# A two-layer graph network kernel: U1 and U2 loaded by SyncE, the activation table loaded ahead, attention sums in groups of two tiles, accumulators taken one by one

## The chip, the cores and the metric

The kernel runs on one core of one Trainium2 chip. The metric is the device time of one execution in microseconds (us), the median of several runs. A profiled execution gives the trace from which single durations are read.

The engines are named as in the profile: PE is TensorE (PEld its weight loads), DVE is VectorE, ACT is ScalarE, POOL is GpSimd, SP is SyncE, which here does nothing but issue DMA transfers. ACT can issue DMAs too (ACTq in the timelines).

## The reference

There are N = 3327 nodes with D = 256 features, an adjacency matrix `adj` (about 0.5% filled, with a full diagonal), and two layers. Each starts with a layer norm and a relu and adds its output to x.

```python
# layer 0, on h = relu(layernorm(x)); Xf = Xa = h, Z = 0
R = adj + I;  R = R / R.sum(-1)
for n in range(2):
    q = Xa @ W1.T @ W2.T;  k = Xa @ W3.T          # 64 wide
    A = softmax(q @ k.T), cut to the largest entries that hold 0.9 of the row, renormalised
    Xf = R @ Xf;  Xa = A @ Xa
    Z += Xf @ U1[n].T + Xa @ U2[n].T
x += layernorm(h + Z) * ln_g + ln_b
# layer 1, on h = relu(layernorm(x)): graph attention, 4 heads of 64 features
hp = h @ W;  s, d = hp @ a_src, hp @ a_dst         # one of each per node and head
e = leaky_relu(s[i] + d[j], 0.2), only where adj[i, j] > 0
x += elu(softmax(e) @ hp)
```

## The kernel before

The rows are padded to 3328 and cut into NT = 26 tiles of 128. The function `fast` does the work; a second path, `general`, is entered only when a check at the end asks for it, which it doesn't for these inputs.

**The order of the work.** Nearly everything goes through a `Plan` (L470 to L567). A step is put into it with `put(engine, length, rank, function, needs, take, give, lag)`: the engine that runs it, an assumed length, a rank (the lowest goes first among the steps that are ready), the steps that it needs, and the buffers that it takes and gives back by name. `order()` plays these steps through as a list schedule on the assumed lengths, and `issue()` then emits the instructions in that order. What comes out is a fixed order for every engine. On the chip each engine runs its list in order, and a wait at the head of the list holds all that stands behind it. A changed rank, length or buffer thus may shift the order anywhere after it.

**The start.** `weights()` (L689 to L726) is called ahead of the plan, and issues on ACT's queue the DMAs of W1 (L696), W2 (L697), W3 twice (L699) and, in a loop over the two steps, the halves of U1 (L702) and U2 (L703), 256 KB each. The tiles of x (128 KB each, L1818) are issued by SP. `deviations` then takes the mean and the variance of each tile on DVE (L1134, L1135) and turns them into scale and offset on POOL (L1139 to L1142). `prepare` follows tile by tile: ACT's relu (L1160, with scale and offset), PE's transposes (L1165), a copy by DVE (L1168), PE's projection on queries and keys (L1173), and ACT's copy of it into a `kq` buffer (L1179; there are three). Out of `kq` POOL copies keys and queries (L1182, L1183) and SP starts a DMA (L1186) that doubles the queries onto other partitions. `keys_summed` (L762 to L783) sums statistics of the keys on PE, DVE and ACT. `project_u` (L1203 to L1215) multiplies every tile by U1 (PE at L1209, four records for a tile), and its two results are copied by ACT (L1212) and DVE (L1213).

**Layer 0.** For each row tile of each step, PE makes logits (L873), ACT their exponents (L887) and a first guess of the threshold (L907 to L910), then `density` (four activations on one column, L914 to L917) and `count` (passes of 3.07 us over 3327 columns, L924). POOL refines the threshold from the counts (`step`, L941 to L970), DVE sorts a window around it and drops what lies below (L979 to L1034), and PE transposes (L1047) and multiplies (L1059) what is left; ACT copies the transposes (L1052). The products with R are made by PE in between (`Full`, L1091), with one PSUM accumulator `accf`, and copied by ACT (L1098). The steps of a row are put into the plan by `search` (L1410 on), where density has the row's rank − 2.05, and the first counts − 2.1.

**Layer 1.** `attend_neighbours` (L1500 to L1811) goes through four blocks of W = 832 target columns. In each block it loops over the 26 source tiles j. ACT makes a 0/1 mask from the adjacency (L1623, L1624), DVE makes the masked exponents of the four heads (L1635, four instructions per tile) into one of seven `e` buffers (four named e, three called e2 in the plan), and PE uses them twice: for the products with the features (L1651, an array tiling of 128×64) into two accumulators of two PSUM banks each (`pl`, all of that pool), and for the sums (L1665, tiling 128×32) into `acca` and `accf`. Sums of JG = 3 tiles are run together after the products of the third. An e buffer is given back by the sums.

At the end of a block, `leave` has ACT copy both accumulators (L1711) and the sums (L1714) into an e buffer. Then seven times PE transposes a piece (L1732), DVE takes the reciprocals (L1736), ACT makes the elu's parts (L1744), and DVE adds (L1748, L1749). Those steps run beside the next block. The next block's first product takes both accumulators and needs `evacuated`, the second of the two copies. The last block ends in a variant of its own.

```python
x_ = plan.put("PE", 1.42, rank, product, 0, needs=[x_, last_acc, evacuated], take=["pl", "pl"] * (j == 0))
last_acc = plan.put("PE", 1.42, rank, product, 1, needs=[x_, y_])
group.append((sums, mine))
if len(group) == JG or j == NT - 1:
    for n_, (fn, name) in enumerate(group):
        last_den = plan.put("PE", 1.42 + 0.2 * (n_ == 0), rank, fn, needs=[last_acc, last_den], ...
```

Of the kernel before, what the change touches and what calls it, by code (L numbers as in the profile page):

```python
# [10 lines left out]
F32 = mybir.dt.float32  # L11
# [3 lines left out]
AF = mybir.ActivationFunctionType  # L15
# [4 lines left out]
P = 128  # L20
# [550 lines left out]
def fast(  # L571
# [17 lines left out]
    nc = tc.nc  # L589
    V, S, T, GP = nc.vector, nc.scalar, nc.tensor, nc.gpsimd  # L590
# [21 lines left out]


    powers = const.tile([P, 4], F32, name="powers")
    adds = const.tile([P, 2], F32, name="adds")
    for k, v in enumerate((-0.5, 0.5, -1.0, 0.25)):
        GP.memset(powers[:, k : k + 1], v)
    for k, v in enumerate(QUANTILE[1:3]):
# [12 lines left out]
    with ExitStack() as l0:  # L631
# [57 lines left out]
        def weights():  # L689
            held = {}  # L690
            w1 = etpool.tile([P, 4, P], F32, name="et")
            w1 = w1[:, 0, :].rearrange("p (c o) -> p c o", c=2)
            w2 = small.tile([P, PIECES, 8], F32, name="cands").rearrange("p c r -> p (c r)")[:DA, :DA]
            w1r = small.tile([P, PIECES * 8], F32, name="rest", bufs=1)[:DA].rearrange("p (k o) -> p k o", k=1)
            w1r = [w1r[:, 0, :], small.tile([P, P], F32, name="kq", bufs=BUFS["kq"])[:DA]]
            nc.scalar.dma_start(w1, w1t.rearrange("(c p) o -> p c o", p=P))  # L696
            nc.scalar.dma_start(w2, w2t)  # L697
            for r in range(2):
                nc.scalar.dma_start(wqk[:, :, r, r * DA : r * DA + DA], w3t.rearrange("(c p) o -> p c o", p=P))  # L699
            for n in range(STEPS):  # L700
                cols = slice((1 - n) * D, (2 - n) * D)
                nc.scalar.dma_start(u1[:, :, cols], u1t[n].rearrange("(c p) o -> p c o", p=P))  # L702
                nc.scalar.dma_start(u2[:, :, cols], u2t[n].rearrange("(c p) o -> p c o", p=P))  # L703

            def turn():
                held["ps"] = ps_x.tile([DA, 2, P], F32, name="px")
                for k in range(2):
                    T.transpose(held["ps"][:, k, :], w1[:, k, :], ident)

            def copy():  # L710
                for k in range(2):
                    S.copy(w1r[k], held["ps"][:, k, :])

            def product():
                held["ps"] = ps_x.tile([P, 2, DA], F32, name="px")
                for k in range(2):
                    T.matmul(held["ps"][:, k, :], w1r[k], w2, start=True, stop=True)

            def place():
                for r in range(2):  # L720
                    S.copy(wqk[:, :, r, (1 - r) * DA : (2 - r) * DA], held["ps"])

            a = plan.put("PE", 0.25, -200.0, turn, take=["px"], needs=[plan.put("SP", 0.02, -201.0, lambda: None, lag=8.0)])
            a = plan.put("ACT", 0.5, -200.0, copy, needs=[a], take=["kq"], give=["px"])
            a = plan.put("PE", 0.25, -200.0, product, needs=[a], take=["px"], give=["kq"])
            return plan.put("ACT", 0.5, -200.0, place, needs=[a], give=["px"])  # L726
# [476 lines left out]
        def project_u(t, rank):  # L1203
            held = {}

            def product():
                ps = held["ps"] = ps_x.tile([P, 2 * D], F32, name="px")
                for k in range(2):
                    T.matmul(ps, c[:, t, k * P : (k + 1) * P], u1[:, k, :], start=(k == 0), stop=(k == 1))  # L1209

            a = plan.put("PE", 1.75, rank, product, needs=[turned_h[t], weighed], take=["px"])
            b = plan.put("ACT", 0.37, -2.6, lambda: S.copy(main[:, t, :D], held["ps"][:, :D]), needs=[a])  # L1212
            e = plan.put("DVE", 0.43, -2.6, lambda: V.tensor_copy(c[:, t, :], held["ps"][:, D:]), needs=[a])  # L1213
            plan.put("SP", 0.0, -2.6, lambda: None, needs=[b, e], give=["px"], lag=0.0)
            return b, e  # L1215
# [194 lines left out]
        def search(row, rank, keys, stats_of, fresh):  # L1410


            n, i = row.n, row.i
            got, a = [], None
            for g in range(2):

                def logits(g=g):
                    row.logits(2 * g)
                    row.logits(2 * g + 1)

                a = plan.put(
                    "PE", 2.1 - 0.7 * g, rank - 2.5, logits, needs=[keys, fresh, a], take=["pl", "pl"] + ["e", "sc"] * (1 - g)
                )
                for k in (2 * g, 2 * g + 1):
                    got.append(
                        plan.put("ACT", 1.15 if k < 3 else 0.5, rank - 2.5, row.exps, k, needs=[a], give=["pl"])
                    )
            row.pieces = dict(logits=a)
            a = plan.put("ACT", 0.35, rank - 2.4, row.row_sum, needs=[got])
            a = plan.put("POOL", 1.3, rank - 2.4, row.root, needs=[a, stats_of])  # L1430
            a = row.pieces["guess"] = plan.put("ACT", 1.0, rank - 2.4, row.guess, needs=[a])
            more = plan.put("ACT", 0.85, rank - 2.05, row.density, needs=[a])
            for j in range(2):
                got = [
                    plan.put("ACT", 3.05, rank - (2.1, 1.7)[j], row.count, j, fn, needs=[a])
                    for fn in (AF.Relu, AF.Sign)[j:]
                ]
                a = plan.put("POOL", (3.8, 4.7)[j], rank - (2.0, 1.6)[j], row.step, j, GP, needs=[got, more])
            if EVALS[n] == 3:
                a = row.pieces["counted"] = plan.put("ACT", 3.05, rank - 1.4, row.count, 2, AF.Sign, needs=[a])  # L1440
                a = plan.put("DVE", 2.7, rank - 1.3, row.step, 2, V, needs=[a])
            halves = []
            for h in range(2):
                for part in range(2):
                    a = plan.put(
                        "DVE", 3.2 - 2.0 * part, rank - 1.0, row.window, h, part, needs=[a], take=["y"] * (1 - part),
                        give=["y"] * part, lag=0.02, hold=1.95 * (1 - part),
                    )
                    halves.append(a)
            may = plan.put("POOL", 0.8, rank - 1.5, row.free, needs=[halves[2]])  # L1450
            a = plan.put("DVE", (1.8, 2.5)[n], rank - 1.0, row.sort, needs=[a])
            a = plan.put("DVE", 3.1, rank - 1.0, row.choose, needs=[a, may], take=["cum"])
            total = plan.put("POOL", 1.2, rank - 1.0, row.total, needs=[a], give=["cum"])
            drops = []
            for o in range(4):
                a = plan.put("DVE", 1.03, rank - 1.0, row.drop, o, needs=[a], hold=1.0)
                drops.append(a)
            return total, drops
# [41 lines left out]
        def attend_neighbours(rows, ends, done, fulls):  # L1500
# [1 line left out]

            W = NP // 4
            C = W // 2
            JG = 3
            logits_done = [r.pieces["logits"] for r in rows]
            freed = [p for p in done]
            extra = {}
# [65 lines left out]

            last, f_ = {}, None
            used_heads = [None, None]
            evacuated = None
            both = broadcast(0, 59.5)
            for b in range(4):
                lo = b * W  # L1580
                r0 = 60.0 + 10.0 * b
                q = {}
                tiles = range(lo // P, lo // P + 7)
                off = lo - tiles[0] * P

                def open_acc(q=q):
                    q["acc"] = [ps_l.tile([P, 2, 512], F32, name="pl") for _ in range(2)]

                def open_den(q=q):
                    q["den"] = [ps_a.tile([P, 512], F32, name=n) for n in ("acca", "accf")]  # L1590
# [3 lines left out]
                for j in range(NT):  # L1594
# [48 lines left out]

                    def product(a, j=j, held=held, q=q, open_acc=open_acc):

                        if j == 0 and a == 0:
                            open_acc()
                        for c in range(2):
                            for k in range(2):
                                h = 2 * a + k  # L1650
# [27 lines left out]
                    else:  # L1678
# [10 lines left out]
                    y_ = plan.put("DVE", 2.1, rank, exponents, 1, needs=[x_, both[1]], give=own, hold=2.0)  # L1689
                    last_e = y_  # L1690
                    x_ = plan.put(
                        "PE", 1.42, rank, product, 0, needs=[x_, last_acc, evacuated], take=["pl", "pl"] * (j == 0)
                    )
                    last_acc = plan.put("PE", 1.42, rank, product, 1, needs=[x_, y_])
                    group.append((sums, mine))
                    if len(group) == JG or j == NT - 1:
                        for n_, (fn, name) in enumerate(group):
# [16 lines left out]
                            S.copy(q["ot"][:, 2, c], q["den"][c][:, :C])  # L1714

                r1 = r0 + 9.0
                evacuated = a = plan.put("ACT", 0.9, r1, leave, 0, needs=[last_acc], take=["e"], give=["pl"])
                evacuated = a = plan.put("ACT", 0.9, r1, leave, 1, needs=[a], give=["pl"])
                out_of = plan.put("ACT", 1.1, r1, leave, 2, needs=[a, last_den], give=["acca", "accf"])
                for x0 in range(0, W, P):  # L1720
                    m = min(P, W - x0, N - lo - x0)
# [95 lines left out]
        def load_x(t):  # L1817
            nc.sync.dma_start(rhs[0][:, t, :], x[t * P : (t + 1) * P, :])  # L1818

        weighed = weights()  # L1820
        loads = [plan.put("SP", 0.58, -200.0 + t, load_x, t) for t in range(NT)]
        measured = {}
# [136 lines left out]
```

## Time and profile before

| | |
|---|---|
| median of 3 runs | 2219.33 us |
| lowest and highest | 2218.48, 2220.72 us |
| profiled execution, its own time | 2222.8 us |
| its span in the trace | 2221.0 us |
| PE busy | 2171.0 us, 98% of the span |
| DVE busy | 1613.7 us, 73% |
| ACT busy | 1442.5 us, 65% |
| POOL busy | 931.3 us, 42% |
| mean granted TensorE clock | 0.998 |

The times in the timelines count from the start of the span. A group's duration is the time from its first start to its last end, so it can hold gaps between its instructions; the ends of matmuls are modelled. The bracket behind an instruction names the idle time of its engine just before, and what ended it. Layer 1's four blocks open on PE at 1720, 1847.90, 1967.31 and 2086.16 us, and the last sums end at 2205.02.

### The profile page before, as it was taken

To read this page: it belongs to the slowest core of one execution; us is meant where nothing else is said; L and a number is where in the kernel's file an instruction comes from. 1 tells how busy PE (TensorE), PEld (TensorE's weight loads), DVE (VectorE), ACT (ScalarE), POOL (GpSimd) and SP (SyncE) were. 2 spreads that over 40 slices of the span, in tenths; PEclk is the share of its full clock that TensorE was granted. 3 is DMA by queue.
4 is the path that set the end of the run, shared out by engine and by line. 5 is a ranking of instruction groups with operands and counts; after the bars stand their busy time and mean duration, and the time that the engine had idled before them with its cause. 6 is when DMAs were issued, how large, how long until landed. Compare 5 with 4: busy or idle time off the path is not lost.

```text
span 2221.0 us, 35941 instructions
## 1 busy us (share of the span) xinstructions
PE 2171.0 (98%) x11978; PEld 1535.2 (69%) x11978; DVE 1613.7 (73%) x4229; ACT 1442.5 (65%) x2725; POOL 931.3 (42%) x2210
## 2 busy tenths in 40 slices
PE   7999999999999999999999999999999999999997
PEld 5388778777887788877878788887887433333333
DVE  5576656546655744277879877888777997989896
ACT  5766676567566661478888777878774455465553
POOL 5564455535544541256656666566653200000001
PEclk9999999999999999999999999999999999999999
DMA  4012121212212232622222222222225344444341
GB/s 120 1 45 80 52 71 54 71 52 62 71 54 71 71 91 67 189 82 60 63 58 63 62 72 74 80 62 64 67 77 152 117 130 143 116 137 126 107 127 50
DMA packets 192323, 183.75 MB, mean 83 GB/s; under 512 B 15386, under 2 KB 146176, under 8 KB 192128
## 3 DMA queue, kind: packets, MB, share of 16 engines
q1 hardware_dynamic: 190144, 180.10, 28.1%
q8 instruction: 96, 1.57, 0.3%
q10 hardware_dynamic: 1984, 1.26, 0.2%
q14 instruction: 99, 0.81, 0.1%
HBM read 164.41 MB, written 15.94 MB: 81 GB/s over the span
## 4 chain that ended last, share of the span: by engine, by line
PE 71%; issue 9%; ACT 8%; POOL 5%; DVE 5%; DMA 2%; SPq 0%; ACTq 0%; DVEq 0%; POOLq 0%
PE acca L1059 20%; PE accf L1091 20%; PE pl L1651 9%; PE pl L873 6%; ACT junk L924 6%; PE px L1047 6%; PE acca L1665 2%; PE accf L1665 2%; PE px L1258 2%; PE px L1209 1%; PE px L1354 1%; POOL sc L937 1%; ACT et L1052 1%; DVE e L1635 1%; PE px L1236 1%
## 5 line engine op out<-in xcount | busy, mean ns | idle before, releaser
L1059 PE MATMUL acca<-rhs,et 128*128 128x256 f32 x2704 | 620.7, 380 | 1.7 <-ACT et L1052 1.6
L924 ACT ACTIVATE junk<-e,sc 128x3327 fp8e5<-128x3327 f32 x182 | 559.1, 3072 | 48.0 <-POOL sc L969 46.6
L1059 PEld LDWEIGHTS acca<-rhs,et 128*128 128x128 f32 x2704 | 499.4, 191 | 66.0 <-ACT et L1052 4.8
L1091 PE MATMUL accf<-c,at 128*128 128x256 f32 x1352 | 313.5, 382 | 6.1 <-ACT f L1098 6.1
L1091 PE MATMUL accf<-main,at 128*128 128x257 f32 x1352 | 310.3, 381 | 3.0 <-DMA at<-in_adjt_dram 2.8
L979 DVE SCALAR_TENSOR_TENSOR y<-e,sc 128x1664 f32<-128x1664 f32 x104 | 208.1, 2001 | 127.1 <-POOL sc L966 125.1
L1052 ACT COPY et<-px 128x512 f32<-128x512 f32 (+1 forms) x364 | 192.6, 553 | 142.0 <-PE acca L1059 83.4
L1091 PEld LDWEIGHTS accf<-c,at 128*128 128x128 f32 x1352 | 250.0, 190 | 48.3 <-ACT f L1098 10.9
L1091 PEld LDWEIGHTS accf<-main,at 128*128 128x128 f32 x1352 | 251.0, 190 | 44.9 <-issue 6.5
L984 DVE MAX8 cands<-y 128x8 f32<-128x208 f32 x832 | 242.4, 361 | 3.6
L1034 DVE SCALAR_TENSOR_TENSOR e<-e,thr 128x832 f32<-128x832 f32 x208 | 212.9, 1079 | 2.0
L887 ACT ACTIVATE e<-pl 128x1024 f32<-128x1024 f32 x208 | 179.0, 863 | 37.6 <-PE pl L873 36.9
L1624 ACT ACTIVATE et<-at 128x448 bf16<-128x448 f32 (+1 forms) x204 | 112.3, 550 | 137.4 <-DVE e L1635 81.6
L1047 PE MATMUL px<-ident,e 128*128 128x128 f32 x1352 | 191.4, 274 | 7.1 <-ACT et L1052 2.3
L1784 POOL TENSOR_TENSOR qq<-qq 128x256 f32<-128x256 f32 x4 | 3.0, 755 | 453.7 <-ACT qq L1780 453.7
L1047 PEld LDWEIGHTS px<-ident,e 128*128 128x128 f32 x1352 | 160.1, 141 | 47.0 <-issue 11.8
L1651 PE MATMUL pl<-e,main 128*64 128x416 f32 x1024 | 187.2, 515 | 0.0
L873 PE MATMUL pl<-kt,qq 64*128 64x512 f32 (+1 forms) x832 | 173.5, 535 | 0.0
L1651 PEld LDWEIGHTS pl<-e,main 128*64 128x64 f32 x1024 | 71.1, 137 | 107.3 <-issue 91.9
L1635 DVE SCALAR_TENSOR_TENSOR e<-c,low,et 128x832 f32<-128x832 f32 x128 | 128.6, 1073 | 7.9 <-PE accf L1665 3.6
L873 PEld LDWEIGHTS pl<-kt,qq 64*128 64x128 f32 x832 | 71.6, 186 | 83.9 <-issue 77.9
L1635 DVE SCALAR_TENSOR_TENSOR e<-qq,low,et 128x832 f32<-128x832 f32 x120 | 120.4, 1076 | 2.6 <-ACT e L1711 2.0
(527 smaller groups left out, 3083.9 us busy)
## 6 DMA issues: line engine op xcount, KB each, us to landing
at<-in_adjt_dram SPq DMA_DIRECT2D x414, 256.0 KB
at<-in_adjt_dram SPq DMA_DIRECT2D x102, 192.0 KB
at<-in_adjt_dram SPq DMA_DIRECT2D x52, 128.0 KB
ys<-ystage SPq DMA_DIRECT2D x26, 256.0 KB
rhs<-in_x_dram SPq DMA_DIRECT2D x26, 128.0 KB
ystage<-in_x_dram SPq DMA_DIRECT2D x26, 128.0 KB
base<-ys SPq DMA_DIRECT2D x26, 128.0 KB
x1s<-ystage SPq DMA_DIRECT2D x26, 128.0 KB
```

The lines of the kernel that those rows point to most:

```text
L873: T.matmul(pl[:, r, :m], qq[half, self.i, :], kt[half, 512 * k : 512 * k + m], start=True, stop=True,)
L887: S.activation(self.e[:, 1024 * k : 1024 * k + 2 * w].rearrange("p (r w) -> p r w", r=2), pl, AF.Exp, accum_out=(self.p0, self.p1, self.p2 ...
L924: S.activation(junk[:, :N], self.e[:, :N], fn, bias=t, scale=-1.0, accum_out=dst, saturate=False)
L979: V.scalar_tensor_tensor(self.y[:, : hi - lo], self.e[:, lo:hi], self.up, self.e[:, lo:hi], ALU.is_lt, ALU.mult, accum_out=(self.h0, self. ...
L984: V.max(self.cands[:, o // PIECE, :], self.y[:, o - lo : min(o + PIECE, hi) - lo])
L1034: V.scalar_tensor_tensor(piece, piece, self.thr[:, o : o + 1], piece, ALU.is_gt, ALU.mult)
L1047: T.transpose(pt[:, k, :], self.e[:, j * P : (j + 1) * P], ident)
L1052: S.copy(self.et[g][:, :m, :], self.pt.pop(g)[:, :m, :])
L1059: T.matmul(self.acc, et[:, j - 4 * g, :], rhs[self.n][:, j, :], start=(j == 0), stop=(j == NT - 1))
L1091: T.matmul(self.acc[:, : self.w], self.at[j // JC][:, j % JC, :], self.src[:, j, : self.w], start=(j == 0), stop=(j == NT - 1),)
L1635: V.scalar_tensor_tensor(held["e"][:, k, :], extra["both"][b % 2][:, k, :], low[:, j, k : k + 1], held["mask"], ALU.max, ALU.mult,)
L1651: T.matmul(q["acc"][a][k * FH : (k + 1) * FH, c, :C], main[:, j, h * FH : (h + 1) * FH], held["e"][:, h, c * C : (c + 1) * C], start=(j == 0),
```

## The change

There are six edits. The loads of U1 and U2 become steps of the plan on SP: U1's two halves with ranks −196.5 and −195.5 among the loads of x (−200 to −175), U2's with rank −150 behind them; `project_u` needs these loads of U1 now and no longer `weighed`, the placing of the projection's weights. ACT gets one activation with Exp on one column straight after its four remaining DMAs, ahead of the plan's steps. Density's rank goes from −2.05 to −2.2. JG goes from 3 to 2. The accumulators are opened, taken and waited for one by one: product 0 of a block's first tile needs the first copy, product 1 the second.

In the order that the plan puts out, SP has four loads of x, U1, one of x, U1, 21 of x, and then U2 twice, ahead of the first doubling DMA. ACT has the four DMAs, the table load, the Exp and then the first relu. In layer 1, blocks 1 to 3 begin with two tiles of products ahead of the first sums, and go on in groups of two.

```diff
-    adds = const.tile([P, 2], F32, name="adds")
+    adds = const.tile([P, 3], F32, name="adds")
@@ weights()
             for n in range(STEPS):
                 cols = slice((1 - n) * D, (2 - n) * D)
-                nc.scalar.dma_start(u1[:, :, cols], u1t[n].rearrange("(c p) o -> p c o", p=P))
-                nc.scalar.dma_start(u2[:, :, cols], u2t[n].rearrange("(c p) o -> p c o", p=P))
+                uloads.append(
+                    plan.put(
+                        "SP", 0.4, -196.5 + n, nc.sync.dma_start, u1[:, :, cols],
+                        u1t[n].rearrange("(c p) o -> p c o", p=P), lag=8.0,
+                    )
+                )
+                plan.put(
+                    "SP", 0.4, -150.0, nc.sync.dma_start, u2[:, :, cols], u2t[n].rearrange("(c p) o -> p c o", p=P)
+                )
+
+            S.activation(adds[:, 2:], powers[:, :1], AF.Exp)
@@ project_u()
-            a = plan.put("PE", 1.75, rank, product, needs=[turned_h[t], weighed], take=["px"])
+            a = plan.put("PE", 1.75, rank, product, needs=[turned_h[t], uloads], take=["px"])
@@ search()
-            more = plan.put("ACT", 0.85, rank - 2.05, row.density, needs=[a])
+            more = plan.put("ACT", 0.85, rank - 2.2, row.density, needs=[a])
@@ attend_neighbours()
-            JG = 3
+            JG = 2
-            evacuated = None
+            evacuated = [None, None]
-                q = {}
+                q = {"acc": {}}
-                def open_acc(q=q):
-                    q["acc"] = [ps_l.tile([P, 2, 512], F32, name="pl") for _ in range(2)]
+                def open_acc(a, q=q):
+                    q["acc"][a] = ps_l.tile([P, 2, 512], F32, name="pl")
-                        if j == 0 and a == 0:
-                            open_acc()
+                        if j == 0:
+                            open_acc(a)
-                        "PE", 1.42, rank, product, 0, needs=[x_, last_acc, evacuated], take=["pl", "pl"] * (j == 0)
+                        "PE", 1.42, rank, product, 0, needs=[x_, last_acc, evacuated[0]], take=["pl"] * (j == 0)
                     )
-                    last_acc = plan.put("PE", 1.42, rank, product, 1, needs=[x_, y_])
+                    last_acc = plan.put(
+                        "PE", 1.42, rank, product, 1, needs=[x_, y_, evacuated[1]], take=["pl"] * (j == 0)
+                    )
-                evacuated = a = plan.put("ACT", 0.9, r1, leave, 0, needs=[last_acc], take=["e"], give=["pl"])
-                evacuated = a = plan.put("ACT", 0.9, r1, leave, 1, needs=[a], give=["pl"])
+                first = plan.put("ACT", 0.9, r1, leave, 0, needs=[last_acc], take=["e"], give=["pl"])
+                a = plan.put("ACT", 0.9, r1, leave, 1, needs=[first], give=["pl"])
+                evacuated = [first, a]
@@ fast()
+        uloads = []
         weighed = weights()
```

## The prediction, made before the result was known

> **What bounds the kernel now.** I read the split of busy time over stretches of the span first. Its columns are the stretch in us, its length, then busy time and instruction count of PE, PEld, DVE, ACT and POOL, then granted clock, DMA share and GB/s. The cuts are the first relu's end on PE (10.76), the first attention (110), layer 1 (1720) and its blocks.
>
> ```profile
> 0.00:10.76 10.76, 0.00 (x0) 0.00 (x0) 2.70 (x10) 1.94 (x3) 5.79 (x33) 1.00 0.77 227
> 10.76:110.00 99.24, 91.68 (x400) 53.38 (x401) 57.46 (x216) 71.41 (x167) 55.12 (x152) 1.00 0.15 43
> 110.00:1720.00 1610.00, 1593.42 (x8089) 1293.03 (x8087) 1103.02 (x3462) 1109.01 (x1938) 852.38 (x2008) 1.00 0.26 73
> 1720.00:1847.90 127.90, 127.28 (x910) 54.44 (x910) 122.49 (x155) 62.84 (x130) 11.88 (x10) 1.00 0.44 130
> 1847.90:1967.31 119.41, 118.05 (x857) 43.84 (x853) 110.18 (x126) 64.88 (x162) 0.00 (x0) 1.00 0.44 130
> ```
>
> TensorE is the bound nearly everywhere: 1593.42 of 1610 us in layer 0's body, 118.05 of 119.41 in block 1. Free time is there in two places: the first 10.76 us, where PE does nothing, and the busy but stretched starts of blocks 1 to 3. So I next read ACT's, POOL's and SP's timelines of the start (start, duration, engine, line; a bracket is idle time and its releaser).
>
> ```profile
> 6.03 0.38 ACTq L702 DMA_DIRECT2D late<-in_u1t_dram  x1
> 8.30 0.40 ACTq L703 DMA_DIRECT2D u<-in_u2t_dram  x1
> 8.81 1.28 ACT L1160 ACT_TABLE_LOAD   x1 [8.81 <-DMA u<-in_u2t_dram]
> 10.11 2.08 ACT L1160 ACTIVATE rhs<-rhs,mvs 128x256 f32<-128x256 f32 x4
> ```
>
> ```profile
> 5.11 0.24 POOL L1142 TENSOR_SCALAR mvs<-mvs 128x1 f32<-128x1 f32 x1
> ```
>
> ```profile
> 0.72 16.47 SPq L1818 DMA_DIRECT2D rhs<-in_x_dram  x26
> 17.44 28.72 SPq L1186 DMA_DIRECT2D qq<-kq  x26
> ```
>
> POOL has tile 0's deviation at 5.35, but ACT's first relu starts at 10.11: it stands behind eight DMAs, of which the last two wait in the queue (6.03, 8.30), and a table load. The third thing to read is PE's and DVE's timeline in layer 1.
>
> ```profile
> 1847.90 2.32 PE L1651 MATMUL pl<-e,main 128*64 128x416 f32 x12
> ...
> 1907.21 5.81 PE L1651 MATMUL pl<-rhs,main 128*64 128x416 f32 x32
> ...
> 1920.07 8.60 PE L1651 MATMUL pl<-e,main 128*64 128x416 f32 x48
> ...
> 1932.93 1.27 PE L1651 MATMUL pl<-c,main 128*64 128x416 f32 x6
> ```
>
> ```profile
> 1860.16 2.08 DVE L1635 SCALAR_TENSOR_TENSOR e<-c,low,et 128x832 f32<-128x832 f32 x2 [1.31 <-PE accf L1665]
> ```
>
> ```profile
> 1978.95 2.08 DVE L1635 SCALAR_TENSOR_TENSOR e<-qq,low,et 128x832 f32<-128x832 f32 x2 [0.59 <-PE accf L1665]
> ```
>
> A cycle of three tiles lasts 1920.07 − 1907.21 = 12.86 us. At a block's start DVE stops for want of an e buffer until the first sums have run.
>
> **What the Trainium skill says.** "ScalarE: Activation LUTs", What ACT_TABLE_LOAD costs: about 1283 ns, and 1380 ns of drain. The trace agrees on the load (1.28 us); it shows no drain behind it, the relu follows in 0.02 us. "DMA: Bandwidth & Descriptors", Issuing engines are not separate DMA queues: transfers from any engine end on the same 16 DMA engines, and moving the issue saves only sequencer time. Here an issue is 0.38 to 0.48 us, but the gaps 6.03 to 8.30 show that ACT stood far longer, so I count the gaps too. "TensorEngine Tiling (Array Packing)", Key Properties: a change of tiling mode drains TensorE. The trace lets me price that below: products are 128×64, sums 128×32.
>
> **The change, part by part.** The profiled execution took 2222.8 us (span 2221.0, 1.8 outside it), 3.5 above the median of 2219.33; I carry differences over unchanged.
>
> *U off ACT, table first.* ACT's queue keeps four weight loads (0.47 + 0.53 + 1.11 us, over by 2.91), the 1.28 load and a [128×1] Exp, about 0.2 (the [128×1] activations L914 to L917 take 0.19 to 0.21). All that ends near 4.5, before POOL's 5.35, so relu 0 goes from 10.11 to about 5.4. Each later step gains less, because each has its own feeder: relus 2 and 3 wait for POOL's 8.63; POOL's next round (12.62, it waited 4.00 for DVE) moves up 4.0. PE could start 4.7 us earlier; that is the upper end. On SP, two U1 DMAs now stand among the x loads, and two U2 DMAs behind them: before the first doubling of the keys (L1186) there are 30 issues in place of 26. The 26 issues of x fill 16.47 us with gaps, as x tiles are awaited too; at the closer spacing of 0.475 us (0.72, 1.18, 1.64, 2.12) the four would cost 1.9 us alone. These doublings hold the three kq buffers for about 2 us each (the first x took from 0.72 to statistics at 3.14, 2.42 us). By hand: U2 issued by 15.8, first doubling about 16.0 and landed at 18.0, in place of 17.44 and the fourth key share (L1179) at 21.29. That gives 3.3 us, which I take: **−3.3**. Lower end: 0, if SP's issues with the U's in them run no faster than now. U1 is first used at 26.33 (L1209) and lands long before.
>
> *Density ahead of the counts.* The diff also moves the rank of density (L914 to L917) below that of the count passes. On ACT four short activations, 67.03 to 67.66, go ahead of a 3.07 us pass. The first row's count then ends 0.6 later, but POOL's step, which waited 1.04 for density at 67.73, need not. So −0.5 to +0.6; taken 0.
>
> *Sums by two tiles.* A tile's products are 16 records, about 2.8 us, its sums 16, about 1.4. A group of three is 12.86, 4.287 a tile. The last group of a block before holds two (26 = 8×3 + 2): 1839.23 to 1847.90 is 8.67, 4.335 a tile. Solving 3t + s = 12.86 and 2t + s = 8.67 gives t = 4.19 and s = 0.29 for one round trip between tilings. Groups per block go from 9 to 13, so 4 × 4 × 0.29 = **+4.6**; counting runs in the emitted order instead, 30 more at 0.147 each, +4.4. I take +4.5. PE is the bound here, nothing hides it: DVE needs 4 × 0.996 = 3.98 us a tile, less than 4.34.
>
> *The block's start.* Of block 1's 119.41 us, products and sums are 26 × 4.19 = 108.9, the 21 transposes 2.3 (six take 0.81 from start to start at 1968.86, with one change of tiling in it), and 28 runs at 0.147 are 4.1: 115.3 in all. The remaining 4.1 is stretch (3.6 in blocks 2 and 3, 118.85 and 118.86 long). Its cause is in the two DVE lines: the fifth exponents start at 1978.95, 11.6 us after the block opened at 1967.31, because the sums which give the first e buffer back were at 1977.28. With groups of two the emitted order has the first sums behind two tiles' products in place of three, by hand 6.7 to 7.2 us after the opening, 3.3 earlier. What comes late next is DVE itself: it has 110.8 us of work per block, against 116 to 117. I leave 1.3 of stall in each: 2.8 + 2.3 + 2.3 = **−7.4**. Bounds: −11.3 (all of it) and 0.
>
> *Accumulators one by one.* The two copies of the accumulators (L1711) run 1843.69 to 1844.54 and 1845.09 to 1845.94, and the sums after the last product hold PE until 1847.90; the next block's first product finds both banks free. With two tiles still 2 × 1.39 = 2.8 us of sums cover them. **0**; if the cover were gone, a copy of 0.85 saved at each of three boundaries, −2.6. Block 0 starts without a stall and stays so, as does the 16 us tail after 2205.02.
>
> *The body.* The planner orders all engines anew, so waits will move. PE idles 16.6 us of 1610 there, most where a copy on ACT is late (6.4 us over 9 waits on L1098). Taken 0, bounds −5 and, below, +11.
>
> Sum: −3.3 + 0 + 4.5 − 7.4 + 0 = −6.2, so 2219.33 − 6.2 = 2213.1 (profiled: 2222.8 to about 2216.6).
>
> **The rivals.** (A) *More of the same*: the stall goes whole (−11.3 + 4.5 = −6.8), and the body's waits may shrink too: 2219.33 − 3.3 − 6.8 = 2209.2, to 2206 with 3 from the body. For it: the body has 16.6 us to give. Against: PE's waits there have several releasers. (B) *Groups of two cost and give nothing*: at the block's start DVE waits next for ACT's elu (a 3.38 us wait on L1744 at 1973.72 is in the trace), the 4.5 us stay: 2219.33 − 3.3 + 4.5 = 2220.5. Against: the e buffer is what was awaited last. (C) *The early start is hidden*: the doublings on SP are no earlier, PE waits for keys: 2219.33 − 2.9 = 2216.4. (D) *Slower*: ACT in the body. A copy (L1098, L1052) that is ordered behind a 3.07 us count pass, because density's new rank shifted the order, holds PE's only accumulator accf. Fourteen more such waits at today's mean of 6.4/9 = 0.7 are +10 and outweigh the 6.2 from the ninth on; with +11 the time is 2224.1. For it: ACT is 69% busy in the body and each of 52 rows is moved. Against: density is a fifth of a pass, and the row's order stays the same.
>
> **How the numbers follow.** About 0.2%, 4.4 us, is what a measurement of this kernel can tell from no change: faster is below 2214.9, slower above 2223.8. Forecast 0.48 (own range 2209 to 2217: 0.34 faster, 0.14 same); A 0.12, all faster; B 0.15 (0.02, 0.11, 0.02 by what the start gives); C 0.12 (0.04, 0.08, 0); D 0.13 (0, 0.01, 0.12). Sums: 0.52, 0.34, 0.14. The range of 2206 to 2222 leaves out D's most and little of A.
>
> **What would show it.** First relu at 5.4 and PE's first matmul near 6; first doubling near 16. In layer 1 a cycle of 8.67 us for two tiles; blocks 1 to 3 near 117.8, 117.7 and 117.7 long; the wait of DVE on accf at a block's start below 1.5 us. I am wrong if blocks exceed 119.4 (B), if attention still begins at 107.5 (C), or if PE's idle time in the body rises above 22 us (D).

## The result, and the profile after

The changed kernel takes 2208.77 us (median of 5 runs, 2207.54 to 2210.26), the kernel before in the same comparison 2220.72 (2218.48 to 2222.51). The ratio is 0.9946 with a 95% interval of 0.9935 to 0.9957: 12.0 us faster, of which the prediction had 6.2. The profiled execution is the median one, 2208.77 us with a span of 2207.0. The profile of before that the prediction worked on, 2222.8, was 2.1 above its kernel's median of now; the trace shows 14.0 us between the two spans for that reason.

Busy time by stretch in the changed kernel, cut at the same events as before (columns: stretch, length, PE, PEld, DVE, ACT, POOL, clock, DMA share, GB/s):

```profile
0.00:5.96 5.96, 0.00 (x0) 0.00 (x1) 1.91 (x7) 2.08 (x3) 3.71 (x27) 1.00 0.61 168
5.96:110.00 104.04, 95.39 (x411) 56.28 (x412) 62.13 (x229) 69.93 (x167) 58.93 (x159) 1.00 0.19 55
...
1838.63:1956.04 117.41, 117.41 (x858) 43.05 (x854) 107.29 (x123) 64.96 (x162) 0.00 (x0) 1.00 0.44 128
1956.04:2073.71 117.67, 117.59 (x858) 42.94 (x854) 109.88 (x126) 65.94 (x164) 0.00 (x0) 1.00 0.42 121
2073.71:2191.38 117.67, 117.59 (x858) 42.95 (x854) 100.71 (x116) 60.21 (x152) 0.00 (x0) 1.00 0.34 97
```

Blocks 1 to 3 last 117.41, 117.67 and 117.67 us, in place of 119.41, 118.85 and 118.86: −4.4 together. Block 1 opens at 1838.63 in place of 1847.90, so 9.3 of the trace's 14.0 us had been gained ahead of it. How much of that was the start, the next two views say. First ACT's timeline at the start, in the changed kernel:

```profile
2.94 1.28 ACT L712 ACT_TABLE_LOAD   x1 [2.94 <-issue]
4.24 0.20 ACT L712 ACTIVATE adds<-powers 128x1 f32<-128x1 f32 x1
5.31 0.60 ACT L1169 ACTIVATE rhs<-rhs,mvs 128x256 f32<-128x256 f32 x1 [0.87 <-POOL mvs L1151]
...
17.15 0.27 ACT L1188 COPY kq<-px 128x128 f32<-128x128 f32 x1 [0.64 <-PE px L1182]
...
20.88 0.46 ACT L1188 COPY kq<-px 128x128 f32<-128x128 f32 x2 [0.71 <-DMA qq<-kq]
```

The relu starts at 5.31 and waits for POOL, as forecast. But the fourth copy into a kq buffer is made at 20.88, where the prediction had 18.0 and the kernel before 21.29. It waits for a doubling DMA. SP's timeline shows when that was issued:

```profile
5.22 10.03 SPq L1830 DMA_DIRECT2D rhs<-in_x_dram  x21
15.29 0.94 SPq L567 DMA_DIRECT2D u<-in_u2t_dram  x2
16.36 27.78 SPq L1195 DMA_DIRECT2D qq<-kq  x26
```

The first doubling leaves at 16.36 (forecast: 16.0) and ACT, at its relus until 20.2, goes on 4.5 us after that. In that stretch the DMA engines are 91% busy and move 272 GB/s:

```profile
16.00:19.50 3.50, 3.46 (x20) 3.14 (x19) 2.03 (x10) 1.61 (x5) 2.25 (x9) 1.00 0.91 272
```

So the doubling waits behind transfers, the last x tiles and 512 KB of U2. Yet the first attention's matmuls (L1068, L1059 before) begin at 108.1 in place of 110.6, −2.5 us. PE's timelines, before and then after:

```profile
110.63 1.89 PE L1059 MATMUL acca<-rhs,et 128*128 128x256 f32 x8
```

```profile
108.07 1.89 PE L1068 MATMUL acca<-rhs,et 128*128 128x256 f32 x8
```

What remains of the 9.3, some 7 us, came from the body of layer 0 and block 0. Part of it belongs to the one execution of before that was profiled: after a wait of PE for 2.08 us its granted clock is 0.50 from 858.3 to 861.7 us, where eight of the attention's products take 3.53 us in place of 1.89. The changed kernel's trace has no such stretch ahead of its last sums. One waits view of PE there (engine and line, what it waited for, sum, count, longest), first before, then after:

```profile
PE accf L1091 <- ACT f L1098: 6.4, 9, 1.8
PE accf L1091 <- DMA at<-in_adjt_dram: 2.8, 2, 1.7
PE px L1047 <- ACT et L1052: 2.3, 4, 1.2
```

```profile
PE accf L1100 <- ACT f L1107: 5.1, 11, 1.1
PE px L1056 <- ACT et L1061: 2.5, 4, 0.8
...
PE accf L1100 <- DMA at<-in_adjt_dram: 0.4, 1, 0.4
```

Several waits are shorter, 2.4 us of it on the adjacency's loads and 1.3 on ACT's copies of f. They are short of 7 us and name no one cause, so the edits had to be tried apart.

### The profile page after: what moved, and what is told of

Read it like the earlier page. It is cut to its first block, busy times and chain, and to the rows that moved or that the text cites. A ratio compares the mean times of both kernels' runs of the same rounds, so it can differ in the third digit from the quotient of the medians.

```text
span 2207.0 us, 35945 instructions
## 1 busy us (share of the span) xinstructions
PE 2169.5 (98%) x11978; PEld 1530.4 (69%) x11978; DVE 1614.3 (73%) x4229; ACT 1443.2 (65%) x2726; POOL 932.8 (42%) x2210
## 5 line engine op out<-in xcount | busy, mean ns | idle before, releaser
L1068 PE MATMUL acca<-rhs,et 128*128 128x256 f32 x2704 | 616.8, 379 | 0.0
L933 ACT ACTIVATE junk<-e,sc 128x3327 fp8e5<-128x3327 f32 x182 | 559.0, 3071 | 68.3 <-POOL sc L978 67.6
L1068 PEld LDWEIGHTS acca<-rhs,et 128*128 128x128 f32 x2704 | 499.3, 190 | 62.5 <-issue 1.5
```

What stands on the lines that cost most here:

```text
L933: S.activation(junk[:, :N], self.e[:, :N], fn, bias=t, scale=-1.0, accum_out=dst, saturate=False)
L1068: T.matmul(self.acc, et[:, j - 4 * g, :], rhs[self.n][:, j, :], start=(j == 0), stop=(j == NT - 1))
```

## The experiments

**Each edit alone.** After the traces were read there were two theories. A: each edit has its own place (U and table at the start, density in the body, groups in the blocks, accumulators nowhere). B: the body's gain comes from any shift of the plan's order. To part them there are four kernels, each the kernel before with one edit.

U and table (the SP loads, the Exp, `uloads` in place of `weighed`):

> Only the U loads on SyncE and the early table load are added to the kernel before. Theory A (each edit has its own place: start, body, blocks): the first attention's transposes move from 107.5 to about 105, the body keeps its idle time of about 17 us on PE and the blocks stay at 119.4, 118.9, 118.9: -2.6 us. Rival B (the body's gain comes from any shift of the plan's order, not from a named edit): the idle time of the body moves by several us here too, so -2.6 with +-5 on it.

Measured: 2218.39 us, ratio 0.9993 (0.9986 to 0.9999), −1.6 us by the ratio. In the profiled execution PE starts 5.0 us earlier, but the first attention begins at 109.8 (110.6 before). It lost time on the way: after a wait of PE for 2.5 us its granted clock is 0.50 from 21.5 to 24.9 us, and 1.00 there in every other trace. Busy time in that stretch, with the columns as above (the clock is the third number from the end):

```profile
19.50:24.00 4.50, 2.83 (x15) 2.83 (x16) 1.38 (x6) 2.08 (x7) 2.04 (x8) 0.72 0.12 29
```

The changed kernel with density's rank put back (a run shown further below) has the same start and no such stretch in it, and begins the first attention at 108.1:

```profile
108.09 1.89 PE L1068 MATMUL acca<-rhs,et 128*128 128x256 f32 x8
```

So the start gives 2.5 us where the clock holds. From 45 us to layer 1 the traces of both show PE, ACT, POOL and DVE in the same order as in the kernel before, and PE's waits in the body name the same releasers in nearly the same sums (6.1 us over 9 on the copies of f, 2.1 on gk). The plan's order held, and rival B fails for this edit. Theory A's 2.6 lies within the interval of the ratio (−3.1 to −0.2 us).

Density's rank:

```diff
-            more = plan.put("ACT", 0.85, rank - 2.05, row.density, needs=[a])
+            more = plan.put("ACT", 0.85, rank - 2.2, row.density, needs=[a])
```

> Only density's rank is lowered (-2.05 to -2.2) in the kernel before. Theory A: the body's gain of about 7 us is density's, because POOL's step no longer waits for it and each row is ready earlier: -5 to -8 us, with PE's idle time in the body down from 17 to about 11 us and blocks unchanged. Rival B: the change is within +-5 us and its sign is open; the body's gain isn't reproduced by this edit alone.

Measured: 2214.07 us, ratio 0.9966 (0.9952 to 0.9979), −7.5 us, all of it ahead of layer 1's blocks, which stay at 119.41, 118.86 and 118.85. This edit, which the title doesn't name, gains the most. Theory A's number is met; what stands behind it was tried below.

Groups of two (`JG = 2`):

> Only JG goes from 3 to 2 in the kernel before. Theory A: blocks 1 to 3 last 117.4, 117.7, 117.7 as in the changed kernel, block 0 about 1.2 longer, so -3.2 us in all, with the cycle of two tiles at 8.67 us. Rival (the blocks' gain needs the accumulators taken one by one): blocks 1 to 3 become longer than 119.4, as the round trips cost 1.2 each and the stall at the block's start stays, +4.5 us. Rival B on the body: layer 0 comes before the sums in rank, so the body's idle time should stay at 17 us until near its end.

Measured: 2217.39 us, ratio 0.9985 (0.9978 to 0.9993), −3.3 us. Blocks 1 to 3 last 117.40, 117.87 and 117.63 without the accumulators' edit. Theory A holds, the rival falls.

Accumulators one by one (`open_acc(a)`, `evacuated = [first, a]`, one `pl` at a time):

> Only the accumulators are taken and waited for one by one in the kernel before. Theory A: nothing, since the sums of the last group cover both copies: 0 within 1 us, blocks at 119.4, 118.9, 118.9. Rival: the first product of a block starts before the last sums and the blocks shorten by up to 0.85 each, -2.6 us.

Measured: 2224.35 us, ratio 1.0020 (1.0014 to 1.0027): 4.4 us slower. Neither the theory nor the rival allowed for a loss. Blocks 2 and 3 last 120.57 in place of 118.85, which is 3.4 of it. DVE's and PE's timelines in block 2 of this kernel show where:

```profile
1985.35 0.18 DVE L1739 RECIPROCAL mv<-px 128x4 f32<-128x4 f32 x1 [1.61 <-PE px L1735]
1985.45 4.04 DVE L1635 SCALAR_TENSOR_TENSOR c<-qq,low,et 128x832 f32<-128x832 f32 x4
```

```profile
1984.77 0.55 PE L1735 MATMUL px<-ident,e 128*128 128x128 f32 x3
1986.56 2.61 PE L1651 MATMUL pl<-c,main 128*64 128x416 f32 x8 [1.24 <-DVE c L1635]
```

In the kernel before, DVE made two of the c exponents ahead of this reciprocal:

```profile
1984.68 2.05 DVE L1635 SCALAR_TENSOR_TENSOR c<-qq,low,et 128x832 f32<-128x832 f32 x2
1986.65 0.18 DVE L1736 RECIPROCAL mv<-px 128x4 f32<-128x4 f32 x1
```

The plan, told that product 1 needs a second wait, put transposes and with them a reciprocal at other places. Now the reciprocal stands ahead of the exponents, waits 1.61 us for PE's transposes, and the exponents behind it leave PE without work for 1.24. The edit only moves the plan, since the chip waited bank by bank already: in the run with groups of two alone, where this edit is not in, the two copies run back to back from 1845.59 to 1847.20, and block 1's first product starts at 1846.85, ahead of the second copy's end. With groups of two in, nothing of the edit shows: the changed kernel's blocks are within 0.2 us of that run's.

The ratios of the three edits that gain multiply to 0.9993 × 0.9966 × 0.9985 = 0.9944; the change measured 0.9946.

**Density: a better place, or another draw of the order?** Each rank or assumed length changes the order that the plan puts out for all engines. To part the two, the assumed length of density (0.85 to 0.6) and of the first counts (3.05 to 3.12) was changed, with density behind and ahead. The instructions are the same in all of them.

```diff
-            more = plan.put("ACT", 0.85, rank - 2.05, row.density, needs=[a])
+            more = plan.put("ACT", 0.6, rank - 2.2, row.density, needs=[a])
```

> The kernel before with density's rank at -2.2 and its assumed length in the plan 0.6 in place of 0.85; the instructions are the same, only the order that the plan puts out differs. Theory M (density ahead of the counts is better by itself): -6 to -7.5 us against the kernel before, as with the rank alone. Rival L (the gain is one draw of the plan's order among many): the gain differs from -7 by several us, anything from -8 to +5.

> The kernel before with density's rank left at -2.05 and only its assumed length 0.6 in place of 0.85. Theory M: 0 within 1.5 us. Rival L: the time moves by several us either way, though nothing of the change is in it.

```diff
-                    plan.put("ACT", 3.05, rank - (2.1, 1.7)[j], row.count, j, fn, needs=[a])
+                    plan.put("ACT", 3.12, rank - (2.1, 1.7)[j], row.count, j, fn, needs=[a])
```

> The kernel before with density's rank left at -2.05 and only the assumed length of the first count passes 3.12 in place of 3.05. Theory M: 0 within 1.5 us. Rival L: the time moves by several us either way.

> Density's rank at -2.2 and the assumed length of the first count passes 3.12. Theory M: -6 to -7.5 us against the kernel before, and as much below the run that has 3.12 with density behind. Rival L: no fixed distance between the two; the scatter of the four orders is as large as the effect.

| assumed lengths (density, count) | density behind | density ahead |
|---|---|---|
| 0.85, 3.05 | the kernel before, 2219.94 (2220.15 beside the other four) | 2214.07, ratio 0.9966 (0.9952 to 0.9979) |
| 0.6, 3.05 | 2215.75, ratio 0.9979 (0.9970 to 0.9987) | 2213.67, ratio 0.9968 (0.9956 to 0.9981) |
| 0.85, 3.12 | 2217.48, ratio 0.9986 (0.9978 to 0.9994) | 2213.04, ratio 0.9962 (0.9947 to 0.9976) |

Neither theory holds whole. With density behind, two changes that mean nothing to the chip gain 4.4 and 2.7 us: the kernel before had the slowest of three orders. With density ahead the three are within about 1 us, and each is faster than its partner, by 5.9, 2.1 and 4.4 (in the middle pair the two intervals overlap). The runs also differ in their mean granted clock, from 0.996 to 0.999; those at 0.998 alone give 6.3, 1.8 and 4.9 (one run for the last), so the clock is not the reason for the difference. So of the gain of some 6 us, about 4 (the mean of the three) goes with the rank, and the rest with the order that the kernel before happened to have; three pairs don't give this closer than to a few us.

How the rank does it stays open. The plain reason would be POOL's wait for density. POOL's waits in the body (110 to 1720) are 22.2 us for it in the kernel before (9.4, 9.1 and 3.7 in the lines below), and none is left with density ahead, in any of the three. There POOL waits for the counts instead (L950 on L933 144.4 us in the changed kernel, the same wait 100.2 before):

```profile
POOL sc L941 <- ACT sc L914: 9.4, 4, 3.6
...
POOL sc L947 <- ACT sc L917: 9.1, 13, 1.8
...
POOL sc L947 <- ACT sc L916: 3.7, 5, 1.1
```

But in the run with the length 0.6 and density behind, the same sum is over twice as large, and that run is 4.4 us faster than the kernel before:

```profile
POOL sc L941 <- ACT sc L914: 30.1, 8, 5.3
...
POOL sc L947 <- ACT sc L917: 8.0, 14, 1.5
...
POOL sc L947 <- ACT sc L916: 6.7, 4, 4.1
...
POOL sc L945 <- ACT sc L914: 4.5, 1, 4.5
```

So POOL's wait for density is not what sets the end. PE's idle time in 110 to 1700 doesn't part the two either: 14.6 us before, 11.8 and 11.4 behind with other lengths, 11.0, 12.6 and 12.1 ahead.

**The rank in the changed kernel.** The changed kernel with density back at −2.05:

> The changed kernel with density's rank back at -2.05. If the rank's gain is one of -6 to -7 in any surroundings: about 2215. If it is about 4 with a scatter of 2 to 3 by the plan's draw, as the runs with other assumed lengths say: 2210 to 2215. If it is a draw alone: 2206 to 2212.

Measured: 2216.11 us, ratio 0.9979 (0.9969 to 0.9988) to the kernel before, so 7.3 above the changed kernel. It is the same pair of orders again as in the first row of the table, and no new draw: from 45 us to layer 1 its trace shows all four engines in the order of the kernel before, and the changed kernel's shows them in that of density alone. The ten runs lie apart by clock: 2216.1 to 2218.7 us at 0.996 and 0.997, 2212.8 to 2215.8 at 0.998 and above. At 0.998 and above the distance to the changed kernel is 5. So a gain of 5 to 7 goes with this pair in two surroundings. The run also says what the change gains without density: 4.7 us by the ratio, of the 6.2 that were forecast.

**The start: is it the transfers?** U2 ranked behind the doublings, in the changed kernel:

```diff
-                    "SP", 0.4, -150.0, nc.sync.dma_start, u2[:, :, cols], u2t[n].rearrange("(c p) o -> p c o", p=P)
+                    "SP", 0.4, -60.0, nc.sync.dma_start, u2[:, :, cols], u2t[n].rearrange("(c p) o -> p c o", p=P)
```

> The changed kernel (2208.8 us) with U2's two loads ranked behind the 26 doubling DMAs. Theory D (the start is held by the transfers: 16 engines over 90% busy until 19.5 us, the first doubling waits behind 512 KB of U2): the first doubling lands about 1.9 us earlier (512 KB at 270 GB/s), the first logits move from 46.9 to 45 or 46, total -1 to -2 us. Rival (the tiles' pipeline of about 1 us each sets when the logits can start): nothing, within 0.5 us, or a small shift of the plan's order.

Measured: 2205.94 us (2204.92 to 2206.28), ratio 0.9932 (0.9918 to 0.9947), 2.8 below the changed kernel's median, though the two intervals overlap a little. The plan puts U2 after three doublings, at the first moment at which SP has nothing else. SP's and ACT's timelines of this kernel:

```profile
15.07 1.82 SPq L1195 DMA_DIRECT2D qq<-kq  x3
16.94 1.09 SPq L567 DMA_DIRECT2D u<-in_u2t_dram  x2
```

```profile
18.46 0.41 ACT L1188 COPY kq<-px 128x128 f32<-128x128 f32 x2
```

The fourth copy into kq is at 18.46, with no wait. With U2 in front it is at 20.4 to 20.9 in four traces, after 0.7 to 2.7 us of waiting for the doubling, so the wait was for U2's transfer. Yet the first logits start at 47.39, not earlier than 46.94: PE took more of the products with U1 in between. The first attention begins at 107.3, in the changed kernel at 108.1, but in the next run, which has the changed kernel's start, at 107.4. So nothing shows that the earlier landing reaches the attention. Some 2 us is gained near 436 us, where the changed kernel has a wait of 2.1 on gk (L792) that is not in this one. Theory D is right on the transfer and not on the gain, which is again the order's.

**Groups of 2, 3, 3, ...** If only the first sums have to be early, the later round trips can be saved:

```diff
-            JG = 2
+            JG = 3
-                    if len(group) == JG or j == NT - 1:
+                    if len(group) == JG or j in (1, NT - 1):
```

> The changed kernel with groups of 2, 3, 3, ... (nine per block, the short one first) in place of thirteen groups of two. Theory (the round trips cost 0.29 each, and only the first group's sums free DVE at a block's start): 4 x 4 x 0.29 = 4.6 us less, blocks 1 to 3 at about 116.2 to 116.5, total about 2204. Rival (groups of three later in the block bring the wait for an e buffer back): blocks 1 to 3 between 117.5 and 119, total 2208 to 2211.

Measured: 2206.84 us, ratio 0.9937 (0.9923 to 0.9951), 1.9 below the changed kernel's median and not to be told from it. Its blocks:

```profile
1837.90:1954.67 116.77, 116.69 (x858) 43.66 (x854) 107.47 (x123) 65.49 (x164) 0.00 (x0) 1.00 0.44 131
1954.67:2072.53 117.86, 117.75 (x858) 44.04 (x854) 109.95 (x126) 66.07 (x164) 0.00 (x0) 1.00 0.42 121
```

Block 1 is 0.6 shorter, block 2 is 0.2 longer. The 1.16 us a block that four round trips cost are saved and given back to stretched products, as PE's timeline of block 2 shows:

```profile
1981.00 6.14 PE L1660 MATMUL pl<-rhs,main 128*64 128x416 f32 x32
1986.64 4.48 PE L1660 MATMUL pl<-e,main 128*64 128x416 f32 x16
```

Sixteen products last 4.48 us there, in place of about 2.9: PE is fed by DVE, which after the block's opening works nearly without a break (110 us in 117.9) and has fallen behind. Block 1 and the total lie between the two theories, blocks 2 and 3 in the rival's range. But the wait that the rival named does not show: DVE's waits in block 2 name ACT's mask (4.8 us) and PE's transposes (2.7), and no sums, which give the e buffers back.

**Both edits.**

> Both edits on the changed kernel: U2 behind the doublings, and groups of 2, 3, 3, ... Theory: the two add, -5.6 to -6.6 us, about 2202.5. Rival: only the groups count, about 2204.

Measured: 2205.44 us (2203.89 to 2205.77), ratio 0.9929 (0.9915 to 0.9943). The two don't add; U2's place alone gives as much. This is the lowest time measured, and not to be told from U2's place alone.

## Why the prediction was right, and where it was off

The direction and the range hold; the gain is twice the forecast. What the sum priced gains 4.7 us of its 6.2 without density (−6.9 to −2.7 by the ratio), and the rest of the gain came from an edit that the sum took at nothing. The range of 16 us holds the time with density's gain and without it (2208.8 and 2216.1), so that it was met is in part luck. By the steps of the sum:

*U off ACT, table first: −3.3 forecast, −1.6 measured by the ratio (−3.1 to −0.2), −2.5 at the first attention.* The size is near, the path was wrong. The relu at 5.3, PE at 5.96, the first doubling at 16.36 are as forecast. The term that failed is "landed at 18.0": it took the landing of a single early x tile, 2 us, for a doubling that stands behind 512 KB of U2 and the last x tiles. It measured 4.5, and the fourth kq copy moved by 0.4 in place of 3.3. The Trainium skill ("DMA: Bandwidth & Descriptors", Issuing engines are not separate DMA queues) was quoted for all DMAs sharing the same 16 engines, and its consequence not drawn: in the kernel before the engines were 98% busy in 4 to 10 us and 91% in 10 to 16 already, so an earlier issue alone could not land much earlier: in the run with groups of two alone, which starts like the kernel before, the first doubling leaves at 17.38 and lets ACT go on at 20.64, with U on SP at 20.4 to 20.9. The gain came another way: by 20 us PE has been busy for 11.7 us in place of 8.5, and from there to the first attention it idles 6.3 in place of 6.9, so that most of its head start stays.

*Density: "−0.5 to +0.6; taken 0", and the body "taken 0".* This is the step that failed. It measured −5.9 by the medians and −7.5 by the ratio, which covers all of the unforecast gain. The working looked at the first row only, and then treated the order of 52 rows as noise around zero. The runs say that the kernel before sat at the slow end of that noise (two meaningless changes gain 2.7 and 4.4), and that the rank adds about 4 beyond it; by which wait stays open.

*Sums by two tiles: +4.5.* Right for the cycle. A cycle of two tiles in the steady part of block 2, in PE's timeline:

```profile
2004.37 3.01 PE L1660 MATMUL pl<-e,main 128*64 128x416 f32 x16
...
2013.03 5.81 PE L1660 MATMUL pl<-rhs,main 128*64 128x416 f32 x32
```

2013.03 − 2004.37 = 8.66, forecast 8.67.

*The block's start: −7.4.* Right. The groups alone measured −3.3, where the sum of the two terms is −2.9, and the blocks are within 0.4 of the 117.8, 117.7, 117.7 that were forecast. The fifth exponents start 8.4 us after the opening (11.6 before):

```profile
1964.46 2.08 DVE L1644 SCALAR_TENSOR_TENSOR e<-qq,low,et 128x832 f32<-128x832 f32 x2 [4.38 <-PE accf L1674]
```

The sign named for it was wrong, though. It said that DVE's wait on accf would be below 1.5 us, and it is 4.38, longer than before. Elu's adds (L1748, L1749) stood ahead of these exponents and filled the time; now they follow. What fell is DVE's waiting in the whole block, from 3.4 + 2.8 + 2.0 + 0.6 = 8.8 to 4.4 + 1.7 + 1.4 = 7.5.

*Accumulators: 0, bounds 0 and −2.6.* Right in the combination, wrong as a bound: alone it is +4.4. The bound left out a loss with the reason that the copies are covered. They are, but the plan was told something else, and reordered two engines.

*The rivals.* Case A (more of the same, 2209) came nearest in time, for a reason that it only touched. D named density's rank as what would make ACT late in the body; the sign was the other one. C had the landing right, hardly earlier than before, but its sign did not come: attention's transposes begin at 105.1, not at 107.5.

## What to carry to other kernels

Where a list schedule orders the engines, an edit has two effects, what it does and how it redraws the order; here the second is worth 2 to 4 us of 2220 either way. Measure it by changing an assumed number that means nothing, and believe a gain of that size only if it outlives several such draws. Look at the granted clock of each trace before two of them are compared to a microsecond. Before a queue is relieved of transfers, look at how busy the DMA engines are in that stretch: if they are full, what counts is which bytes go first. And follow a gain up to the work that bounds the kernel: here a wait for a transfer went away, and the first attention was no earlier for it.

## What the runs showed of the hardware

One round trip between 128×64 products and 128×32 sums costs about 0.3 us on PE, an estimate from cycles of 12.86 us for three tiles and 8.66 for two. At the start 16 engines moved 262 to 292 GB/s at 91 to 96% busy (4 to 19.5 us of the changed kernel), and a 32 KB transfer issued behind 512 KB took 4.5 us to let its waiter go. The drain of 1380 ns that the Trainium skill ("ScalarE: Activation LUTs", What ACT_TABLE_LOAD costs) gives beside the load of 1.28 us did not appear: the Exp starts at 4.24, 0.02 us after the load.

In the 14 traces PE has 13 gaps of 2.1 to 4.7 us between its first work and the last sums. In nine of them the granted clock falls to 0.50, 2.2 to 3.4 us after the gap began, and stays there for 3.4 us (6.8 in one). After the gaps of 1.9 us and less it never does.
